# One set of 15 tiles for depthwise sums and products, TensorE's conv in bands 1, 3, 5 of the first six, and places of their own for the first two bands

## The chip, the cores and the metric

The kernel runs on one core of one Trainium2 chip. Five engines work side by side, each with a queue of its own that is executed in order: TensorE (PE, with weight loads shown apart as PEld), VectorE (DVE), ScalarE (ACT), GpSimd (POOL) and SyncE (SP); 16 DMA engines move data. The metric is the device time of one execution in microseconds, the median of the runs.

## What is computed

One block of an image transformer: a channel attention per image and a feed-forward part with a depthwise 3x3 convolution, both behind a layer norm over the channels, both added to their input. x is 16 images of 128 channels and 96 x 96 pixels, float32; HID is 512.

```python
def _attention(xn, wq, wk, wv, wp):
    q, k, v = xn @ wq.T, xn @ wk.T, xn @ wv.T      # split into 8 heads of 16 channels
    q, k = _l2norm(q), _l2norm(k)                  # over the pixels
    attn = softmax(einsum('bhcn,bhdn->bhcd', q, k) * scale, axis=-1)
    out = einsum('bhcd,bhdn->bhcn', attn, v)
    return out @ wp.T

def _ffn(xn_nchw, w_in, w_dw, w_out):
    h1 = einsum('bchw,oc->bohw', xn_nchw, w_in[:, :, 0, 0])
    h2 = conv3x3_depthwise(h1, w_dw, padding=1)    # 512 channels, a 3x3 kernel for each
    h3 = gelu(h2, approximate=False)
    return einsum('bchw,oc->bohw', h3, w_out[:, :, 0, 0])

x = x + _attention(_layernorm(x, ln1_w, ln1_b))
x = x + _ffn(_layernorm(x, ln2_w, ln2_b))
```

## The kernel before

**Tiling.** Channels lie on the 128 partitions. An image is cut into 24 units of four rows (384 pixels, three tiles of 128 pixels), 12 loads of eight rows, and 6 bands of 16 rows; there are 96 bands in all. The hidden 512 channels are four chunks of 128 (n = 0 to 3).

**Norms and attention.** Each norm transposes tiles of 128 pixels (L635), takes statistics on DVE (L642), variance and power -0.5 on POOL (L649, L653), for the second norm a shift on DVE (L657), normalises from PSUM into zT (L689, L693, ACT; for the first tiles of the first image half of it on DVE, L676, L680) and transposes back (L740) into a ring of rows, `xn` (L744, L746). The first norm also sums a Gram matrix (L703), from which `attention` makes one 128 x 128 matrix per image. The second norm of an image starts with `x2`: a matmul with that matrix (mix, L584), a copy with a bias (mixed, L593), and a DMA that adds the image's input (L596, add_x); the result is stored to the output (store_x2, L599, on SP).

**Feed-forward.** For each band and chunk there is a job (`conv_job`): hidden rows by matmuls in chunks of four or five rows (L915), copied from PSUM by ACT (kept, L918; the two rows shared with the next band by halo, L910); six of the nine taps on DVE, the first starting from the centre row (L939, tap); the two other taps as products on ACT (L932), each into a tile `pr`, the second added to the first by an accumulating DMA and the sum to the job's h3 tile by another (both L946, add_last and add_first, issued by POOL); then a GELU on ACT (L950). The last job of the kernel does all its taps on DVE. In 45 of the 96 bands the chunk n = 3 is not such a job: PE computes it straight from the ring with nine matmuls per strip of four rows (`by_matmuls`, L1004, conv), and ACT takes the GELU from PSUM (L1010, conv_gelu). Which bands these are is said by `by_pe`; in the first image they are bands 0, 2 and 4. `ffn_out` multiplies each strip of the four h3 tiles with w_out (L1028, out). ACT copies the sum into the h3 tile of chunk 3 (L1038, evicted), and a DMA adds it to the output (L1042, add_out); in the last two bands DVE adds it in SBUF instead (L1035, add) and SP stores it (L1052).

**What sets the order.** The instructions are not issued in the order of the loops. Every operation is entered in a `Plan` with its engine, an assumed duration, a place (a number in units of jobs: where it belongs by its band or pixel, plus an offset by kind from the table `AT`; the suffix `_0` marks offsets for the first image), and its reads and writes. `Plan.order` then plays the program through: whenever an engine is free, of its ready operations for which there is buffer space the one with the lowest place is taken. The order of starts is the order in which the instructions are written into the engines' queues. Since the offsets reach hundreds of jobs (the kernel has 339), most of them work as a rank among the kinds of an engine. `SLACK`, `WAIT`, `T_ADD` and `T_MOVE` are assumed latencies and transfer times: an accumulating DMA is taken to occupy the DMA engines for T_ADD[0] + rows * T_ADD[1] ns, one after the other.

**Buffers.** Pools are counted in the plan: two PSUM tiles for transposes (tr), four PSUM banks (h) for hidden, conv, mix and out, ten tiles h3 and five tiles pr of 128 x 1536 float32 (6 KB on each partition), four x tiles (xb), three x1. A pool named in IN_TURN gives its buffers only in the order of the places of the operations that take them first; in another pool any ready operation takes a free one.

Of the kernel before, what the change touches and what calls it, by code (L numbers as in the profile page):

```python
# [18 lines left out]
BR = 16  # L19
# [4 lines left out]
PE_LAST = (0, 1, 3, 4)  # L24
TINY = 1e-20
# [6 lines left out]
X1_BUFS, XB_BUFS, PR_BUFS, H3_BUFS, ZT_BUFS = 3, 4, 5, 10, 3  # L32
X0_BUFS = 3
LAST_ADDS = 2
IN_TURN = ("tr", "h3", "pr", "xb", "x1")
AT = dict(
    load_1=-82.1, load_2=-27.85, tables=-170.8, weights=-129.7, zeros=-5.45, load_a=-119.45, forth_a=-5.4,
    stats_a=-130.1, variance_a=-36.15, power_a=-38.2, scaled_a=-151.9, gram=7.8, back_a=-100.3, place_a=-166.4,
    attention=-123.25, mix=-101.45, residual=124.95, mixed=-106.55, add_x=-178.75, forth_b=-9.85,
    stats_b=-312.0, variance_b=594.35, power_b=241.0, shift_b=-51.85, scaled_b=-63.5, back_b=3.3, place_b=-6.65,  # L40
    evicted=-118.4, add_out=244.25, halo=-36.95, hidden=4.7, kept=-139.55, products=-75.8, add_last=43.35,
    tap=6.95, add_first=132.2, gelu=234.35, conv=3.75, conv_gelu=5.75, out=8.15, add=-100.45, store=85.05,
    mix_0=-101.6, residual_0=-64.15, mixed_0=101.1, add_x_0=77.55, gram_0=-52.6, forth_a_0=-54.45,
    forth_b_0=-9.0, stats_a_0=-275.15, stats_b_0=-308.15, scaled_a_0=-213.65, scaled_b_0=-68.05, back_a_0=-91.7,
    back_b_0=-101.3, place_a_0=-91.65, place_b_0=135.9, shift_b_0=-192.4, late=27.25, store_x2=34.35,
    store_x2_0=129.2, variance_a_0=-27.2, variance_b_0=76.25, power_a_0=-38.75, power_b_0=-6.8,
    attention_0=-133.2, load_a_0=-414.85,
)
STEP = dict(scaled=0.3, hidden=0.1, products=0.5, tap=0.166, conv=1.6, conv_tap=0.03, out=0.8, out_part=0.05)
SLACK = dict(PE=200, DVE=0, ACT=150, POOL=0, ADD=890, MOVE=800)  # L50
# [6 lines left out]
T_ADD, T_MOVE = (460.32, 221.76), 121  # L57
# [157 lines left out]
def tile_restormer_block(  # L215
# [171 lines left out]
    def add(p, f, r, w, n=BR):  # L387
        op("POOL", 800, p, f, r, w, 350 + SLACK["ADD"], dma=T_ADD[0] + n * T_ADD[1])
# [505 lines left out]
    def conv_job(j, g, n):  # L894
# [34 lines left out]
        def product(t):  # L929
            o0, o1 = reach(t)  # L930
            d["pr", t] = prp.tile([P, BR, W], F32, tag="pr", name=f"pr_{g}_{n}_{t}")
            nc.scalar.activation(d["pr", t][:, o0:o1, :], shifted(t, o0, o1), AF.Copy, scale=ratio[:, n, t : t + 1])  # L932
# [24 lines left out]
        for k, (r, e) in enumerate(chunks):  # L957
            ph = ("h", (jn, r))
            jk, zs = j + STEP["hidden"] * k, z_units(i, r0 - 1 + r, r0 - 1 + e)
            to = [("h1", n, k)]  # L960
            if r < 2:
                to.append(("h1", n, "first"))
            if e > BR:
                to.append(("h1", n, "last"))
            pe(t_mm((e - r) * W), at("hidden", jk), lambda r=r, e=e: hidden(r, e), [*zs, ("w", "in")], [ph])
            act(t_copy((e - r) * W), at("kept", jk), lambda r=r, e=e: kept(r, e), [ph], to)
        for k, t in enumerate(dma_taps):
            jk = j + STEP["products"] * k
            act(t_act(BR * W, 1), at("products", jk), lambda t=t: product(t), h1, [("pr", (jn, t))])
        pr = [("pr", (jn, t)) for t in dma_taps]  # L970
        for k, t in enumerate(dma_taps[1:]):
            add(at("add_last", j), lambda t=t: add_products(t), [pr[1 + k]], [pr[0]])
        for k, t in enumerate(left):
            o0, o1 = reach(t)
            dve(t_dve((o1 - o0) * (W if k == 0 or t % 3 == 1 else W - 1)), at("tap", j + STEP["tap"] * k), lambda t=t: tap(t), [*h1, ("w", "pads")], h3, True)
        if dma_taps:
            add(at("add_first", j), lambda: add_products(dma_taps[0]), [pr[0]], h3)
        if to_halo:
            act(t_copy(2 * W) + 44, at("halo", j), halo, [("h1", n, "last")], [("h1", n, "first")])
        for s in range(0, UPB, 1 if last else UPB):  # L980
            e = s + 1 if last else UPB
            act(t_act((e - s) * UT), at("gelu", j), lambda s=s, e=e: gelu(s, e), [], h3[s:e])

    def by_matmuls(p, g, s):
# [27 lines left out]
        for k, t in enumerate(order):  # L1012
            o0, o1 = reach(t)
            zs = z_units(i, r0 + o0 + t // 3 - 1, r0 + o1 + t // 3 - 1)
            ns = t_mm((o1 - o0) * (W - (t % 3 != 1)))
            pe(ns, at("conv", p + STEP["conv_tap"] * k), lambda t=t: product(t), [*zs, ("w", "conv")], [pc])
        act(t_act(UT), at("conv_gelu", p), gelu, [pc], [("h3", (g, PE_CHUNK), s)])

    def ffn_out(p, g, s):
# [34 lines left out]
        for k, n in enumerate(order):  # L1054
            pk = p + STEP["out_part"] * k
            pe(t_mm(UT), at("out", pk), lambda k=k, n=n: product(k, n), [("h3", (g, n), s), ("w", "out")], [po])
        if g < NG - LAST_ADDS:
            act(t_copy(UT), at("evicted", p), evicted, [po], [("h3", (g, PE_CHUNK), s)])
# [11 lines left out]
    def by_pe(g):  # L1070
        k = NG - 1 - g
        return k in PE_LAST if k < NB else (k + 1) * PE_SHARE[0] // PE_SHARE[1] > k * PE_SHARE[0] // PE_SHARE[1]
# [14 lines left out]
    for i in range(B):  # L1087
        start2 = job_of(NB * i - 1)
        end1 = start2 - NORM1_END
        start1 = job_of(NB * (i - 1)) if i else end1 - 8  # L1090
# [40 lines left out]
```

## Time and profile before

| | |
|---|---|
| time, median of 3 runs | 4080.88 us (4080.79 to 4082.98) |
| the profiled execution | 4089.63 us, of which the traced span is 4087.9 us |
| mean granted TensorE clock | 0.998 |
| DMA moved | 829.50 MB, mean 203 GB/s |

Groups of instructions are shown as "line engine op, output<-input, shapes, count | busy us in total, mean ns of one | idle time of the engine just before them, and what ended most of it". Matmuls of float32 are two instructions each; a busy PE is not PE at its peak, since their ends are modelled. In a timeline each row is a start, a length, an engine and a run of like instructions; a bracket gives idle time just before it and what ended that. An idle engine that doesn't set the pace costs nothing.

### The profile page before, as it was taken

What the parts mean: (1) busy time and instruction counts of PE and PEld (TensorE: products, weight loads), DVE (VectorE), ACT (ScalarE), POOL (GpSimd) and SP (SyncE); (2) the same over time, 40 slices, a digit from 0 to 9 for tenths busy, and PEclk for the clock granted to TensorE, in tenths of its full rate; (3) what the DMA queues carried; (4) which work ended last, traced back from release to release, by engine and by line L of the source; (5) the groups of instructions that cost most, each with busy time, mean ns of one, the idle gap of its engine ahead of it and who ended that gap; (6) DMA issues with size and microseconds to landing.
All of it is one profiled execution on the core that took longest, in us unless ns stands there. A gap on an engine that the chain in (4) does not pass through costs nothing. (4 is left out here: it accounts for less than half of the span.)

```text
span 4087.9 us, 50655 instructions
## 1 busy us (share of the span) xinstructions
PE 4025.0 (98%) x17209; PEld 2631.0 (64%) x17209; DVE 3967.9 (97%) x3773; ACT 3586.6 (88%) x6678; POOL 2659.8 (65%) x2166
## 2 busy tenths in 40 slices
PE   8999999999999999999999999999999999999999
PEld 6666666566666665666666666666666666666665
DVE  5999999999999999999999999999999999999999
ACT  5989989898899989988989898998989989899974
POOL 4657757576675767857677575765757757576631
PEclk9999999999999999999999999999999999999999
DMA  4989999998999999999999999999999999999987
GB/s 127 205 180 220 199 223 208 194 221 186 214 209 207 219 189 230 200 204 220 185 229 198 207 217 201 216 202 202 221 194 221 205 216 212 194 218 191 215 168 151
DMA packets 196291, 829.50 MB, mean 203 GB/s; under 512 B 22720, under 2 KB 24256, under 8 KB 196032
## 3 DMA queue, kind: packets, MB, share of 16 engines
q0 software_dynamic: 138096, 674.43, 85.0%
q1 hardware_dynamic: 55584, 151.02, 10.3%
q8 instruction: 137, 2.24, 0.2%
q10 hardware_dynamic: 2352, 0.81, 0.1%
q14 instruction: 122, 1.00, 0.1%
HBM read 150.62 MB, written 149.42 MB: 73 GB/s over the span
## 5 line engine op out<-in xcount | busy, mean ns | idle before, releaser
L939 DVE SCALAR_TENSOR_TENSOR h<-h,ratio,h 128x1520 f32<-128x1520 f32 (+1 forms) x1697 | 2988.1, 1779 | 3.6
L1004 PE MATMUL h<-xn,comp 128*128 128x380 f32 (+3 forms) x3294 | 1144.5, 477 | 2.8 <-ACT xn L744 0.9
L1028 PE MATMUL h<-h,woutT 128*128 128x384 f32 x3072 | 1126.5, 488 | 7.2 <-ACT h L918 3.7
L932 ACT ACTIVATE pr<-h,ratio 128x1536 f32<-128x1536 f32 (+1 forms) x676 | 1079.6, 1603 | 19.6 <-DMA h<-pr 10.6
L915 PE MATMUL h<-xn,winT 128*128 128x384 f32 (+3 forms) x2698 | 1052.7, 494 | 6.3 <-ACT h L918 4.5
L1004 PEld LDWEIGHTS h<-xn,comp 128*128 128x128 f32 x3294 | 593.3, 190 | 334.0 <-issue 18.2
L1028 PEld LDWEIGHTS h<-h,woutT 128*128 128x128 f32 x3072 | 557.4, 190 | 350.7 <-issue 41.8
L918 ACT COPY h<-h 128x384 f32<-128x384 f32 (+1 forms) x1307 | 661.3, 537 | 108.3 <-PE h L915 97.1
L915 PEld LDWEIGHTS h<-xn,winT 128*128 128x128 f32 x2698 | 484.2, 190 | 277.3 <-issue 21.3
L939 DVE SCALAR_TENSOR_TENSOR h<-h,ratio 128x1536 f32<-128x1536 f32 x339 | 613.8, 1813 | 15.7 <-PE h L1028 9.4
L653 POOL TENSOR_TENSOR rstd_b<-ve_b,mhalf 128x4 f32<-128x4 f32 x288 | 588.6, 2044 | 14.3
L653 POOL TENSOR_TENSOR rstd_a<-ve_a,mhalf 128x4 f32<-128x4 f32 x288 | 563.4, 1956 | 14.6
L649 POOL TENSOR_SCALAR ve_a<-st_a 128x4 f32<-128x4 f32 x288 | 369.1, 1282 | 292.9 <-DVE st_a L642 226.6
L950 ACT ACTIVATE h<-h 128x1536 f32<-128x1536 f32 x342 | 520.9, 1524 | 24.7 <-DMA h<-pr 23.1
L649 POOL TENSOR_SCALAR ve_b<-st_b 128x4 f32<-128x4 f32 x288 | 386.7, 1343 | 218.4 <-DVE st_b L642 196.9
L946 POOL DMA_DIRECT2D h<-pr x338 | 328.8, 973 | 293.0 <-DVE h L939 98.2
L946 POOL DMA_DIRECT2D pr<-pr x338 | 310.7, 920 | 296.6 <-ACT pr L932 255.2
L693 ACT ACTIVATE zT<-pT_b,nb_b,rstd_b 128x128 f32<-128x128 f32 x1132 | 433.2, 487 | 39.1 <-DVE nb_b L657 38.4
L689 ACT ACTIVATE zT<-pT_a,rstd_a 128x128 f32<-128x128 f32 x1080 | 319.4, 415 | 33.5 <-POOL rstd_a L653 32.6
L703 PE MATMUL g<-zT 128*128 128x129 f32 x2304 | 306.5, 276 | 0.0
L703 PEld LDWEIGHTS g<-zT 128*128 128x128 f32 x2304 | 289.1, 192 | 23.6 <-ACT zT L689 0.4
L584 PE MATMUL h<-xn,mwT 128*128 128x384 f32 x768 | 281.8, 491 | 7.5 <-ACT x L593 3.0
(172 smaller groups left out, 3660.0 us busy)
## 6 DMA issues: line engine op xcount, KB each, us to landing
h<-pr POOLq DMA_DIRECT2D x338, 768.0 KB, 10.3
pr<-pr POOLq DMA_DIRECT2D x226, 768.0 KB, 7.8
pr<-pr POOLq DMA_DIRECT2D x112, 720.0 KB, 14.1
x<-in_x_dram SPq DMA_DIRECT2D x192, 384.0 KB, 7.5
out_dram<-x SPq DMA_DIRECT2D x190, 384.0 KB, 10.1
x<-in_x_dram POOLq DMA_DIRECT2D x189, 384.0 KB, 11.9
out_dram<-h POOLq DMA_DIRECT2D x94, 768.0 KB, 10.6
out_dram<-x SPq DMA_DIRECT2D x4, 192.0 KB, 1.9
```

The source lines that it names most:

```text
L649: nc.gpsimd.tensor_scalar(ve, d["mv"][:, :, 2], 1.0 / C, EPS, ALU.mult, ALU.add)
L653: nc.gpsimd.tensor_tensor(rstd, d["ve"], mhalf, ALU.pow)
L693: nc.scalar.activation(zT(q)[:, k, :P], d["pT", q][:, k, :], AF.Identity, bias=d["nb"][:, t : t + 1], scale=d["rstd"][:, t : t + 1],)
L703: nc.tensor.matmul(grams[i][:, : P + 1], lhsT=zt[:, :P], rhs=zt, start=(q == 0 and k == 0), stop=(q == NU * TPU // QT - 1 and k == QT - 1),)
L915: nc.tensor.matmul(rows(ph)[:, k : k + m, :], lhsT=winT[:, n, :], rhs=z, start=True, stop=True)
L918: nc.scalar.copy(window(h1_, r, e - r, 1), rows(d.pop(("ph", r))))
L932: nc.scalar.activation(d["pr", t][:, o0:o1, :], shifted(t, o0, o1), AF.Copy, scale=ratio[:, n, t : t + 1])
L939: nc.vector.scalar_tensor_tensor(h3[:, o0:o1, w0:w1], shifted(t, o0, o1, w0, w1), ratio[:, n, t : t + 1], onto, ALU.mult, ALU.add)
L946: nc.gpsimd.dma_start(out=to[:, o0:o1, :], in_=d["pr", t][:, o0:o1, :], accum_op=ALU.add)
L950: nc.scalar.activation(h3, h3, AF.Gelu)
L1004: nc.tensor.matmul(d["pc"][:, o0 + k : o0 + k + m, w0:w1], lhsT=comp[:, t, :], rhs=z[:, :, w0 + dx : w1 + dx], start=(t == order[0]), stop ...
L1028: nc.tensor.matmul(rows(d["po"]), lhsT=woutT[:, n, :], rhs=h3s[g, n][:, s * UR : (s + 1) * UR, :], start=(k == 0), stop=(k == NCH - 1),)
```

## The change

It has four parts.

- In the first image PE's conv takes chunk 3 of bands 1, 3 and 5 in place of 0, 2 and 4 (`PE_FIRST`). The number of jobs stays 339.
- The pool of five pr tiles and that of ten h3 tiles become one pool of 15 h3 tiles, and it is no longer given out in the order of places.
- Nearly all offsets in `AT` change, and the feed-forward operations of the first two bands (g < HEAD) get offsets of their own with the suffix `_0`.
- The plan's assumptions change: SLACK of ACT, of accumulating DMAs (ADD) and of SP's transfers (MOVE), T_ADD, and 1000 ns in place of 800 for POOL's issue of an accumulating DMA.

No operation is added or removed.

```diff
 PE_CHUNK = 3
 PE_SHARE = (9, 20)
 PE_LAST = (0, 1, 3, 4)
+PE_FIRST = [1, 3, 5]
+HEAD = 2
+LATE1 = 0.0
 TINY = 1e-20
 UNIT_MIN = 1e-18
 DMA_TAPS = (1, 7)
...
 CENTRE = 4
 QT, QB = 4, 1
 H_BANKS = 4
-X1_BUFS, XB_BUFS, PR_BUFS, H3_BUFS, ZT_BUFS = 3, 4, 5, 10, 3
+X1_BUFS, XB_BUFS, PR_BUFS, H3_BUFS, ZT_BUFS = 3, 4, 1, 15, 3
 X0_BUFS = 3
 LAST_ADDS = 2
-IN_TURN = ("tr", "h3", "pr", "xb", "x1")
+IN_TURN = ("tr", "xb", "x1")
 AT = dict(
-    load_1=-82.1, load_2=-27.85, tables=-170.8, weights=-129.7, zeros=-5.45, load_a=-119.45, forth_a=-5.4,
-    stats_a=-130.1, variance_a=-36.15, power_a=-38.2, scaled_a=-151.9, gram=7.8, back_a=-100.3, place_a=-166.4,
-    attention=-123.25, mix=-101.45, residual=124.95, mixed=-106.55, add_x=-178.75, forth_b=-9.85,
-    stats_b=-312.0, variance_b=594.35, power_b=241.0, shift_b=-51.85, scaled_b=-63.5, back_b=3.3, place_b=-6.65,
-    evicted=-118.4, add_out=244.25, halo=-36.95, hidden=4.7, kept=-139.55, products=-75.8, add_last=43.35,
-    tap=6.95, add_first=132.2, gelu=234.35, conv=3.75, conv_gelu=5.75, out=8.15, add=-100.45, store=85.05,
-    mix_0=-101.6, residual_0=-64.15, mixed_0=101.1, add_x_0=77.55, gram_0=-52.6, forth_a_0=-54.45,
-    forth_b_0=-9.0, stats_a_0=-275.15, stats_b_0=-308.15, scaled_a_0=-213.65, scaled_b_0=-68.05, back_a_0=-91.7,
-    back_b_0=-101.3, place_a_0=-91.65, place_b_0=135.9, shift_b_0=-192.4, late=27.25, store_x2=34.35,
-    store_x2_0=129.2, variance_a_0=-27.2, variance_b_0=76.25, power_a_0=-38.75, power_b_0=-6.8,
-    attention_0=-133.2, load_a_0=-414.85,
+    load_1=117.1, load_2=143.85, tables=-90.8, weights=18.65, zeros=101.15, load_a=-110.6, forth_a=-4.4,
+    stats_a=-54.7, variance_a=-15.2, power_a=121.8, scaled_a=-832.95, gram=7.8, back_a=-123.35, place_a=78.25,
+    attention=-115.7, mix=-2.85, residual=-48.0, mixed=-106.15, add_x=-52.8, forth_b=-9.5, stats_b=-178.0,
+    variance_b=-93.15, power_b=-47.35, shift_b=90.8, scaled_b=-166.1, back_b=-51.15, place_b=-212.9,
+    evicted=1.25, add_out=92.9, halo=34.6, hidden=4.7, kept=-294.4, products=307.15, add_last=75.85, tap=316.95,
+    add_first=-144.65, gelu=229.4, conv=3.75, conv_gelu=253.7, out=8.15, add=555.9, store=147.4, mix_0=-129.1,
+    residual_0=-149.05, mixed_0=-89.75, add_x_0=29.65, gram_0=-91.9, forth_a_0=-192.4, forth_b_0=-8.45,
+    stats_a_0=-99.25, stats_b_0=-42.7, scaled_a_0=133.65, scaled_b_0=75.55, back_a_0=21.3, back_b_0=-233.8,
+    place_a_0=267.85, place_b_0=69.05, shift_b_0=-143.8, late=-172.4, store_x2=51.6, store_x2_0=72.7,
+    variance_a_0=-138.3, variance_b_0=12.35, power_a_0=169.5, power_b_0=-18.55, attention_0=-140.55,
+    load_a_0=-272.4, hidden_0=4.4, kept_0=-89.45, products_0=420.1, tap_0=24.0, add_last_0=374.45,
+    add_first_0=538.6, gelu_0=117.7, conv_0=3.15, conv_gelu_0=85.25, out_0=8.15, evicted_0=71.15,
 )
 STEP = dict(scaled=0.3, hidden=0.1, products=0.5, tap=0.166, conv=1.6, conv_tap=0.03, out=0.8, out_part=0.05)
-SLACK = dict(PE=200, DVE=0, ACT=150, POOL=0, ADD=890, MOVE=800)
+SLACK = dict(PE=200, DVE=0, ACT=100, POOL=0, ADD=770, MOVE=920)
 NORM1_END = 6.0
 EARLY = 5
 WAIT = dict(POOL=700, SP=1800, ACT=1800)
 T_WEIGHTS = 3000
 T_VARIANCE = 250
 T_POWER = 1010
-T_ADD, T_MOVE = (460.32, 221.76), 121
+T_ADD, T_MOVE = (456.21, 219.78), 121
 
 
 class Plan:
...
         op("POOL", ns, p, f, r, w, ns + 33 + SLACK["POOL"])
 
     def add(p, f, r, w, n=BR):
-        op("POOL", 800, p, f, r, w, 350 + SLACK["ADD"], dma=T_ADD[0] + n * T_ADD[1])
+        op("POOL", 1000, p, f, r, w, 350 + SLACK["ADD"], dma=T_ADD[0] + n * T_ADD[1])
 
     def move(p, f, r, w, n=XR):
         op("SP", 60, p, f, r, w, 350 + SLACK["MOVE"], dma=n * T_MOVE)
...
 
         def product(t):
             o0, o1 = reach(t)
-            d["pr", t] = prp.tile([P, BR, W], F32, tag="pr", name=f"pr_{g}_{n}_{t}")
+            d["pr", t] = h3p.tile([P, BR, W], F32, tag="h3", name=f"pr_{g}_{n}_{t}")
             nc.scalar.activation(d["pr", t][:, o0:o1, :], shifted(t, o0, o1), AF.Copy, scale=ratio[:, n, t : t + 1])
 
         def tap(t):
...
                 to.append(("h1", n, "first"))
             if e > BR:
                 to.append(("h1", n, "last"))
-            pe(t_mm((e - r) * W), at("hidden", jk), lambda r=r, e=e: hidden(r, e), [*zs, ("w", "in")], [ph])
-            act(t_copy((e - r) * W), at("kept", jk), lambda r=r, e=e: kept(r, e), [ph], to)
+            pe(t_mm((e - r) * W), at("hidden", jk, g >= HEAD), lambda r=r, e=e: hidden(r, e), [*zs, ("w", "in")], [ph])
+            act(t_copy((e - r) * W), at("kept", jk, g >= HEAD), lambda r=r, e=e: kept(r, e), [ph], to)
         for k, t in enumerate(dma_taps):
             jk = j + STEP["products"] * k
-            act(t_act(BR * W, 1), at("products", jk), lambda t=t: product(t), h1, [("pr", (jn, t))])
-        pr = [("pr", (jn, t)) for t in dma_taps]
+            act(t_act(BR * W, 1), at("products", jk, g >= HEAD), lambda t=t: product(t), h1, [("h3", ("pr", jn, t))])
+        pr = [("h3", ("pr", jn, t)) for t in dma_taps]
         for k, t in enumerate(dma_taps[1:]):
-            add(at("add_last", j), lambda t=t: add_products(t), [pr[1 + k]], [pr[0]])
+            add(at("add_last", j, g >= HEAD), lambda t=t: add_products(t), [pr[1 + k]], [pr[0]])
         for k, t in enumerate(left):
             o0, o1 = reach(t)
-            dve(t_dve((o1 - o0) * (W if k == 0 or t % 3 == 1 else W - 1)), at("tap", j + STEP["tap"] * k), lambda t=t: tap(t), [*h1, ("w", "pads")], h3, True)
+            dve(t_dve((o1 - o0) * (W if k == 0 or t % 3 == 1 else W - 1)), at("tap", j + STEP["tap"] * k, g >= HEAD), lambda t=t: tap(t), [*h1, ("w", "pads")], h3, True)
         if dma_taps:
-            add(at("add_first", j), lambda: add_products(dma_taps[0]), [pr[0]], h3)
+            add(at("add_first", j, g >= HEAD), lambda: add_products(dma_taps[0]), [pr[0]], h3)
         if to_halo:
             act(t_copy(2 * W) + 44, at("halo", j), halo, [("h1", n, "last")], [("h1", n, "first")])
         for s in range(0, UPB, 1 if last else UPB):
             e = s + 1 if last else UPB
-            act(t_act((e - s) * UT), at("gelu", j), lambda s=s, e=e: gelu(s, e), [], h3[s:e])
+            act(t_act((e - s) * UT), at("gelu", j, g >= HEAD), lambda s=s, e=e: gelu(s, e), [], h3[s:e])
 
     def by_matmuls(p, g, s):
 
...
             o0, o1 = reach(t)
             zs = z_units(i, r0 + o0 + t // 3 - 1, r0 + o1 + t // 3 - 1)
             ns = t_mm((o1 - o0) * (W - (t % 3 != 1)))
-            pe(ns, at("conv", p + STEP["conv_tap"] * k), lambda t=t: product(t), [*zs, ("w", "conv")], [pc])
-        act(t_act(UT), at("conv_gelu", p), gelu, [pc], [("h3", (g, PE_CHUNK), s)])
+            pe(ns, at("conv", p + STEP["conv_tap"] * k, g >= HEAD), lambda t=t: product(t), [*zs, ("w", "conv")], [pc])
+        act(t_act(UT), at("conv_gelu", p, g >= HEAD), gelu, [pc], [("h3", (g, PE_CHUNK), s)])
 
     def ffn_out(p, g, s):
         i, b = divmod(g, NB)
...
 
         for k, n in enumerate(order):
             pk = p + STEP["out_part"] * k
-            pe(t_mm(UT), at("out", pk), lambda k=k, n=n: product(k, n), [("h3", (g, n), s), ("w", "out")], [po])
+            pe(t_mm(UT), at("out", pk, g >= HEAD), lambda k=k, n=n: product(k, n), [("h3", (g, n), s), ("w", "out")], [po])
         if g < NG - LAST_ADDS:
-            act(t_copy(UT), at("evicted", p), evicted, [po], [("h3", (g, PE_CHUNK), s)])
+            act(t_copy(UT), at("evicted", p, g >= HEAD), evicted, [po], [("h3", (g, PE_CHUNK), s)])
             if s == UPB - 1:
                 cs = range(b * BR // XR, (b + 1) * BR // XR)
                 add(at("add_out", p), add_out, [("h3", (g, PE_CHUNK), k) for k in range(UPB)], [("o", i, c) for c in cs])
...
 
     def by_pe(g):
         k = NG - 1 - g
+        if g < NB:
+            return g in PE_FIRST
         return k in PE_LAST if k < NB else (k + 1) * PE_SHARE[0] // PE_SHARE[1] > k * PE_SHARE[0] // PE_SHARE[1]
 
     jobs, first = [], []
...
     for i in range(B):
         start2 = job_of(NB * i - 1)
         end1 = start2 - NORM1_END
-        start1 = job_of(NB * (i - 1)) if i else end1 - 8
+        start1 = job_of(NB * (i - 1)) + (LATE1 if i == 1 else 0) if i else end1 - 8
         norm(i, False, lambda t: start1 + (end1 - start1) * t / (NU * TPU))
         attention(at("attention", start2, i), i)
         norm(i, True, lambda t: start2 + band * t / TPB)
```

## The prediction

> **What bounds the kernel now.** I read the page's engine rows first, then the busy time of the engines in five stretches and two short ones near the end (columns: window, length, then PE, PEld, DVE, ACT and POOL busy with instruction counts, granted clock, DMA share, GB/s).
>
> ```profile
> PE 4025.0 (98%) x17209; PEld 2631.0 (64%) x17209; DVE 3967.9 (97%) x3773; ACT 3586.6 (88%) x6678; POOL 2659.8 (65%) x2166
> ```
>
> ```profile
> 0.00:60.00 60.00, 47.49 (x334) 43.25 (x335) 35.92 (x129) 22.42 (x65) 24.73 (x76) 0.95 0.39 113
> 60.00:100.00 40.00, 37.13 (x164) 23.64 (x164) 22.65 (x48) 28.00 (x59) 19.46 (x27) 0.99 0.61 144
> 100.00:3950.00 3850.00, 3810.19 (x16299) 2487.84 (x16298) 3780.90 (x3517) 3459.07 (x6449) 2595.45 (x2041) 1.00 0.98 207
> 3950.00:4050.00 100.00, 98.52 (x317) 57.89 (x316) 99.93 (x59) 69.43 (x98) 17.53 (x21) 1.00 0.84 162
> 4050.00:4088.00 38.00, 31.71 (x100) 18.39 (x98) 28.46 (x23) 7.67 (x10) 2.59 (x3) 1.00 0.52 119
> ```
>
> ```profile
> 3800.00:3900.00 100.00, 100.00 (x374) 61.68 (x373) 98.84 (x96) 86.60 (x157) 71.16 (x55) 1.00 1.02 215
> 3900.00:3950.00 50.00, 50.00 (x180) 30.96 (x179) 41.84 (x34) 41.90 (x66) 24.04 (x20) 1.00 0.92 182
> ```
>
> Three resources are nearly full at once from 100 to 3950 us: PE is idle for 3850 - 3810.2 = 39.8 us, DVE for 3850 - 3780.9 = 69.1 us, and the DMA engines are busy 0.98. The change keeps the number of PE's bands (three of the first six, 45 of 96 in all), so all three keep their work, and what can be won is idle time only: those 39.8 us of PE, the start (12.5 us of PE idle to 60, 2.9 to 100, but 17.4 of DVE in 60 to 100) and 6.3 us of PE at the end. From 3900 to 3950 DVE is idle 8.2 us beside a full PE, so close to the end it is PE that sets the pace.
>
> Then the waits (engine and line, what it waited for: total us, times, longest).
>
> ```profile
> POOL pr L946 <- ACT pr L932: 255.2, 127, 11.1
> ACT zT L693 <- DVE nb_b L657: 38.4, 46, 3.2
> ACT h L950 <- DMA h<-pr: 23.1, 10, 13.5
> DVE nb_b L657 <- POOL rstd_b L653: 21.7, 26, 1.9
> ACT pr L932 <- DMA h<-pr: 10.6, 13, 2.2
> DVE h L939 <- PE h L1028: 9.4, 4, 5.0
> ACT pr L932 <- DMA pr<-pr: 6.7, 10, 1.6
> ```
>
> The idle time is in small pieces. Waits for a buffer are the last three: products waiting for one of five product tiles (10.6 + 6.7 us of ACT) and first taps waiting until the output matmuls gave back an h3 tile (9.4 us of DVE). The one steady loss that POOL's order makes on DVE is the 21.7 us for rstd_b.
>
> The duration rows used below:
>
> ```profile
> L939 DVE SCALAR_TENSOR_TENSOR h<-h,ratio,h 128x1520 f32<-128x1520 f32 (+1 forms) x1697 | 2988.1, 1779 | 3.6
> L932 ACT ACTIVATE pr<-h,ratio 128x1536 f32<-128x1536 f32 (+1 forms) x676 | 1079.6, 1603 | 19.6 <-DMA h<-pr 10.6
> L653 POOL TENSOR_TENSOR rstd_b<-ve_b,mhalf 128x4 f32<-128x4 f32 x288 | 588.6, 2044 | 14.3
> L946 POOL DMA_DIRECT2D h<-pr x338 | 328.8, 973 | 293.0 <-DVE h L939 98.2
> ```
>
> **The change, part by part.** First, bands 1, 3, 5 instead of 0, 2, 4 for PE's conv. Band 0 gains a fourth DVE job: six taps of about 1.78 us (10.7 us of DVE), two products (3.2 us of ACT), two accumulating DMAs (two issues of 0.97 us on POOL), four more hidden matmul pairs. It gives up 36 conv matmuls of two instructions each, which band 1 takes; the same swap is made between bands 2 and 3 and between 4 and 5. The sum is nil; the place is not. From the timelines of PE, ACT and DVE at the start:
>
> ```profile
> 75.81 1.78 PE L1004 MATMUL h<-xn,comp 128*128 128x384 f32 x6
> 86.90 0.97 PE L915 MATMUL h<-xn,winT 128*128 128x480 f32 x2
> 88.77 2.20 PE L915 MATMUL h<-xn,winT 128*128 128x384 f32 x6 [0.46 <-ACT h L1010]
> ```
>
> ```profile
> 69.08 0.58 ACT L744 ACTIVATE xn<-pB_b,b 128x384 f32<-128x384 f32 x1
> 70.39 0.58 ACT L744 ACTIVATE xn<-pB_b,b 128x384 f32<-128x384 f32 x1
> 72.49 0.57 ACT L744 ACTIVATE xn<-pB_b,b 128x384 f32<-128x384 f32 x1
> 74.55 0.57 ACT L744 ACTIVATE xn<-pB_b,b 128x384 f32<-128x384 f32 x1
> 78.12 0.58 ACT L744 ACTIVATE xn<-pB_b,b 128x384 f32<-128x384 f32 x1 [0.15 <-PE pB_b L740]
> 89.98 0.61 ACT L744 ACTIVATE xn<-pB_b,b 128x384 f32<-128x384 f32 x1
> 96.35 0.69 ACT L744 ACTIVATE xn<-pB_b,b 128x384 f32<-128x384 f32 x1
> ```
>
> ```profile
> 91.77 1.82 DVE L939 SCALAR_TENSOR_TENSOR h<-h,ratio 128x1536 f32<-128x1536 f32 x1 [2.66 <-ACT h L918]
> ```
>
> A job of band 0 needs z rows 0 to 17, five units of four rows; the fifth L744 ends at 78.12 + 0.58 = 78.7. Yet PE's first hidden matmul starts at 86.9, behind conv matmuls of band 0 that began at 75.81, and its second chunk waits for the bank that the conv's GELU (L1010) reads. The first tap follows 4.87 us after the first hidden matmul. Without the conv in front, the same chain from 78.7 gives a first tap at 83.6: DVE, and with it the first products and DMAs, start 8.2 us earlier. That is the gain's end. The other end: PE loses the filler that it had before 100 us, L1004 for 12.21 us:
>
> ```profile
> 60.00:100.00 40.00, 12.21 (x36) 0.99 0.61 144
> ```
>
> What covers it is hidden work of band 0 (four jobs of four chunks, some 10.5 us, by 0.97 + 2.20 us in the rows above for a first job with its waits) and the conv strips of band 1 as their units arrive. If that cover fails, 12.2 us are lost. Since PE, not DVE, paces the end, a head start of DVE counts in part only: -3, between -8.2 and +12.2.
>
> Second, the end. Only two bands keep their output sums in SBUF, added by DVE (L1035). Those adds had place -100 and now have 555.9, behind the taps' 316.95.
>
> ```profile
> 4059.51 0.55 DVE L1035 TENSOR_TENSOR x<-h,x 128x384 f32<-128x384 f32 x1
> 4066.82 0.55 DVE L1035 TENSOR_TENSOR x<-h,x 128x384 f32<-128x384 f32 x1
> 4068.90 0.55 DVE L1035 TENSOR_TENSOR x<-h,x 128x384 f32<-128x384 f32 x1
> 4072.69 0.55 DVE L1035 TENSOR_TENSOR x<-h,x 128x384 f32<-128x384 f32 x1
> 4073.16 7.05 DVE L939 SCALAR_TENSOR_TENSOR h<-h,ratio,h 128x1425 f32<-128x1425 f32 x4
> 4081.81 1.85 DVE L1035 TENSOR_TENSOR x<-h,x 128x384 f32<-128x384 f32 x3 [1.61 <-PE h L1028]
> ```
>
> Four adds stand between the last job's taps, each pushing the next tap by about 0.47 us (4059.51 to 4059.98 in start times); moved behind the taps, they fill the gap of 1.61 us before 4081.81. That saves 4 x 0.47 = 1.9 us. The wait it can add: a sum that isn't added holds one of four PSUM banks, and PE's last output matmuls queue behind it. Bounds: the whole PE idle time after 4050, -6.3, and the same again lost. I take -2.
>
> Third, one set of 15 tiles, taken by whoever is ready, not in the order of places. It can remove the three buffer waits. ACT's 17.3 us lie beside 12% of idle ACT time and are worth nothing alone; DVE's 9.4 us are worth up to themselves. What it can add: products made early may hold tiles that first taps want, and the tap, its later taps, the GELU and the output matmuls stand behind it. One such wait is 9.4 / 4 = 2.35 us; one in every tenth of the 339 jobs would be 34 x 2.35 = 80 us, the other end. I take -4, since 15 shared tiles admit every split that 10 and 5 did.
>
> Fourth, the places. On POOL the variance of the second norm goes from last (594) to near the front (-93), its power from 241 to -47, and the first norm's power goes last (121.8). This works on the 21.7 us of DVE and, through nb_b, on the 38.4 us of ACT. The first-add DMAs move from 132 to the very front (-144.65). Each waits for a job's last tap, and variances, powers and the other DMAs stand behind it in POOL's queue, with ACT's normalising behind those; but a place chooses among ready operations only, so this costs where the chip is later than the plan, and POOL is idle a third of the time. On ACT the products go from the middle (-75.8) to last (307); the accumulating DMAs, the taps' completion and the GELU come after them. Bounds: -21.7 from POOL's order; for ACT's order, DMA share falling from 0.98 to 0.97 over 3850 us, 39 us. I take -6, nearer to nothing, because the products' lateness shows today only on POOL (255.2 us), which has slack. On PE the mix goes from -101.45 to -2.85 and the back transposes of the second norm from 3.3 to -51.15: the same instructions later or earlier among others that keep PE full, so nothing. SP keeps its order, loads ahead of stores. The planner's own numbers (slack, transfer times, 1000 ns instead of 800 per issue beside 973 ns measured) issue nothing and act through the order alone.
>
> **Sum.** -3 - 2 - 4 - 6 = -15 us on the profiled execution's 4089.63 us (span 4087.9), so 4074.6. The median of the runs, 4080.88, lies 8.75 us below the profiled time; the same offset gives 4066.
>
> A rule of the Trainium skill speaks to the first term (Perfetto Trace Analysis, Identifying the Most-Contended Engine): TensorE's headroom is judged by weight-load busy time, not by matmul busy time. By it PE at 64% would have a third to spare, DVE would be the bound, and the whole head start of 8.2 us would count: 4061. The trace shows what 64% is here:
>
> ```profile
> 4063.22 13.06 PE L1028 MATMUL h<-h,woutT 128*128 128x384 f32 x40
> L1028 PEld LDWEIGHTS h<-h,woutT 128*128 128x128 f32 x3072 | 557.4, 190 | 350.7 <-issue 41.8
> ```
>
> 40 matmuls without a gap take 13.06 us, 0.33 us each, with one load of 0.19 us each: 58% load share in a stretch where PE is full. So I keep -3.
>
> **Rivals.** (a) Larger gain: shared tiles and POOL's order remove half of the steady idle time. Half of PE's 39.8 us is 20, with 8 at the start and 2 at the end 30: 4051. For it, the waits are short and many; against it, they have many causes, of which the change touches four.
>
> (b) No change: band 0's lost filler shows in full and PE carries it to the end. The first part then costs its +12.2 us, the other three give -12: 4081. For it: PE paces the end. Against it: before 60 us PE was idle 12.5 us anyway for the chain of the first image, and the sixth and seventh units, which open the first two strips of band 1's conv, were there at 90.6 and 97.0 us already. A second mechanism lends it something: powers run faster while no taps run,
>
> ```profile
> 65.00 1.01 POOL L653 TENSOR_TENSOR rstd_b<-ve_b,mhalf 128x4 f32<-128x4 f32 x1
> ```
>
> against 2.04 us on average. Taps that start earlier slow the four batches that band 1's units 5 to 8 need (tiles 15 to 26, four to a batch) by 1.03 us each: 4.1 us later z rows, and by this alone 4066 + 4 = 4070, inside the forecast's own range. The Trainium skill names this as a lock on a port pair shared by VectorE and GpSimd, for VectorE instructions with two SBUF inputs too (SBUF — State Buffer, SBUF: two separate sides). It speaks against starting taps earlier, and the two durations agree with it.
>
> (c) Slower: ACT's products at the back of its queue. DMA is the third full resource and is fed only through products, which now yield to each gather of GELUs, evictions and norm scalings. Point from which it decides: the DMA share from 100 to 3950 falls by 0.01 or more without the span having been bound elsewhere; each 0.01 is 38.5 us. One hundredth, with 5 us of start and end gained: 4114. For it: ACT is 90% busy there, so last in its order means long delays, and POOL waits for products 127 times already. Against it: five tiles of lead become up to fifteen.
>
> **Chances.** Forecast (4055 to 4073) 0.40, (a) 0.17, (b) 0.18, (c) 0.25. This kernel can tell 0.2%, 8.2 us: faster is below 4072.7 and slower above 4089.0. Forecast and (a) are faster, 0.57; (b) is the same, 0.18; (c) is slower, 0.25. The likeliest case's own range is 4055 to 4073. To leave out no more than two in ten I go down to 4040, past (a)'s value, and up to 4108, most of the way to one lost hundredth of DMA share.
>
> **What would show it.** First part: first L939 at or before 85 us, first L1004 after 85. Second: no L1035 between the last job's taps. Third: DVE h waiting for PE h L1028 near nothing, and no new wait of DVE for an output or a transfer. Fourth: DVE nb_b waiting for rstd_b well below 21.7, DMA share still 0.98. Together: PE idle from 100 to 3950 below 30 us. A DMA share of 0.97, or more than 69 us of DVE idle there, would prove me wrong.

## The result, and the profile after

The changed kernel takes 4129.37 us (median of 4 runs, 4127.2 to 4136.93) beside 4080.84 us for the kernel before in the same runs: a ratio of 1.0123, with a 95% interval of 1.0106 to 1.0141. It is 48.5 us slower, where 15 us faster was forecast, and lies above the stated range, which ended at 4108. Its profiled execution took 4128.37 us, of which the span is 4126.6.

The engine row of the page and the busy time by stretches of the kernel after (windows placed as before, the end later):

```profile
PE 4046.3 (98%) x17209; PEld 2638.8 (64%) x17209; DVE 3968.6 (96%) x3773; ACT 3586.9 (87%) x6678; POOL 2595.2 (63%) x2166
```

```profile
0.00:60.00 60.00, 48.29 (x322) 42.18 (x323) 37.20 (x132) 20.16 (x59) 24.49 (x76) 0.89 0.38 113
60.00:100.00 40.00, 37.69 (x164) 23.69 (x163) 30.14 (x50) 32.78 (x67) 23.10 (x25) 0.96 0.66 159
100.00:3950.00 3850.00, 3787.93 (x16164) 2470.52 (x16163) 3737.34 (x3484) 3423.06 (x6392) 2508.12 (x2026) 1.00 0.97 205
3950.00:4090.00 140.00, 139.28 (x460) 82.86 (x459) 139.79 (x91) 104.78 (x154) 37.00 (x39) 1.00 0.87 167
4090.00:4127.00 37.00, 33.08 (x105) 19.50 (x103) 24.18 (x20) 6.16 (x9) 2.51 (x3) 1.00 0.50 117
```

The work is the same (instruction counts agree on every engine). The start is better: DVE is idle 9.9 us from 60 to 100, not 17.4. The time is lost in the long middle stretch: there DVE is idle 3850 - 3737.3 = 112.7 us (69.1 before) and PE 62.1 us (39.8 before). PE's busy time over the whole run has grown by 21 us with the same matmuls, and the granted clock was lower (0.993 on average, 0.998 before): 4126.6 x 0.007 less 4087.9 x 0.002 is 21 us of clock, the same amount. The loss is not spread evenly. Two windows hold a good part of it:

```profile
2000.00:2100.00 100.00, 93.09 (x333) 55.88 (x333) 91.44 (x83) 84.32 (x141) 47.78 (x43) 0.95 1.02 215
...
2900.00:3000.00 100.00, 90.70 (x398) 60.80 (x398) 88.63 (x83) 81.45 (x157) 60.63 (x51) 0.95 0.93 202
```

The waits of DVE and of ACT's products in the kernel after say what is new (L943 is the tap, L936 the product, L646 the statistics, L639 the transpose before them, L661 the shift nb_b; they were L939, L932, L642, L635 and L657):

```profile
DVE st_b L646 <- PE pT_b L639: 28.7, 42, 3.8
...
ACT pr L936 <- DMA pr<-pr: 23.2, 11, 6.7
DVE st_a L646 <- PE pT_a L639: 22.5, 25, 7.2
...
DVE h L943 <- DMA h<-pr: 14.8, 6, 6.2
...
DVE nb_b L661 <- POOL rstd_b L657: 11.5, 15, 1.9
...
DVE h L943 <- DMA pr<-pr: 9.1, 3, 6.1
```

Before, no tap ever waited for a DMA. Now nine do, for 23.9 us in all. The products' waits for DMAs between product tiles (pr<-pr) have grown from 6.7 to 23.2 us, and the longest from 1.6 to 6.7. One of the taps' waits shows what such a wait drags along. POOL's, DVE's, ACT's and PE's timelines around 2064 us of the kernel after:

```profile
2059.01 0.92 POOL L950 DMA_DIRECT2D pr<-pr  x1 [0.43 <-ACT pr L936]
```

```profile
2064.66 1.82 DVE L943 SCALAR_TENSOR_TENSOR h<-h,ratio 128x1536 f32<-128x1536 f32 x1 [6.08 <-DMA pr<-pr]
2066.40 1.79 DVE L943 SCALAR_TENSOR_TENSOR h<-h,ratio,h 128x1520 f32<-128x1520 f32 x1
2068.11 0.15 DVE L661 SCALAR_TENSOR_TENSOR nb_b<-st_b,rstd_b 128x4 f32<-128x4 f32 x1
```

```profile
2068.30 1.50 ACT L697 ACTIVATE zT<-pT_b,nb_b,rstd_b 128x128 f32<-128x128 f32 x4 [3.14 <-DVE nb_b L661]
```

```profile
2068.81 0.82 PE L744 MATMUL pB_b<-ident,zT 128*128 128x128 f32 x2 [2.06 <-ACT zT L697]
```

A first tap waits 6.08 us for a DMA issued at 2059.01. Behind it in DVE's queue, after one more tap, stands the small shift nb_b. For that, ACT's normalisation waits 3.14 us, and for the normalisation PE waits 2.06 us.

A product's wait drags along as much. Two of them, and the matmul on PE that came next, from the timelines of ACT and PE in the kernel after:

```profile
2375.91 1.50 ACT L936 ACTIVATE pr<-h,ratio 128x1440 f32<-128x1440 f32 x1 [5.02 <-DMA pr<-pr]
2377.91 1.65 PE L919 MATMUL h<-xn,winT 128*128 128x384 f32 x2 [4.57 <-ACT h L922]
```

```profile
2927.86 1.57 ACT L936 ACTIVATE pr<-h,ratio 128x1536 f32<-128x1536 f32 x1 [6.72 <-DMA pr<-pr]
2930.51 1.11 PE L639 MATMUL pT_b<-ident,x 128*128 128x128 f32 x4 [7.20 <-ACT zT L693]
```

Behind such a product in ACT's queue stand the copies (L922) and normalisations (L693) for which PE waits. A third case ends at 2676.51, with a wait of 5.56 us on ACT and of 4.54 us on PE. These are the three longest pauses of PE from 100 to 3950 us, 16.3 us together, where PE's idle time there has grown by 22 us.

Why should a first tap wait for a DMA that reads a product tile? A tap writes a fresh h3 tile. Which memory it gets is decided in two places: the plan counts free tiles by the time at which it reckons their last user done, and the tile pool of the language then assigns the memory itself. Counted in the two built programs: before, all 1071 tiles of this kind follow the same tile in their memory as in the plan; after, 447 do not. For three first taps with a wait of 6 us (the 20th, the 168th, which is the one above, and the 239th):

```
first tap of     the plan: memory of     the program: memory of
h3, band 5, n 1     h3, band 3, n 0         pr, band 4, n 2
h3, band 47, n 0    h3, band 45, n 1        pr, band 47, n 0
h3, band 67, n 0    h3, band 65, n 0        pr, band 66, n 1
```

The tap of band 47 was given the memory of its own job's second product, whose accumulating DMA had just been issued; the plan had meant a tile freed long before. In 964 of 1056 cases the pool's choice is the free tile whose last user stands earliest in the program. So it goes, in nine cases of ten, by position in the program, where a DMA stands at its issue, and not by the time at which it lands. With ten h3 and five pr tiles apart and in the order of places, both rules gave the same answer; in one shared set they do not.

### The profile page after: what moved, and what is told of

It reads as the page before. It is cut to its first block, busy times and chain, and to the rows that moved or that the text cites. A ratio compares the mean times of both kernels' runs of the same rounds, so it can differ in the third digit from the quotient of the medians.

```text
span 4126.6 us, 50740 instructions
## 1 busy us (share of the span) xinstructions
PE 4046.3 (98%) x17209; PEld 2638.8 (64%) x17209; DVE 3968.6 (96%) x3773; ACT 3586.9 (87%) x6678; POOL 2595.2 (63%) x2166
## 4 chain that ended last, share of the span: by engine, by line
PE 68%; DVE 10%; ACT 10%; DMA 7%; POOL 3%; issue 2%; ACTq 0%; POOLq 0%; DVEq 0%
PE h L1008 18%; PE h L1032 17%; PE h L919 14%; DVE h L943 9%; PE g L707 5%; DMA pr<-pr 4%; PE h L588 3%; ACT pr L936 3%; DMA h<-pr 2%; PE pB_a L744 2%; PE pT_a L639 2%; PE pT_b L639 2%; PE pB_b L744 2%; ACT h L922 2%; ACT zT L697 1%
## 5 line engine op out<-in xcount | busy, mean ns | idle before, releaser
L943 DVE SCALAR_TENSOR_TENSOR h<-h,ratio,h 128x1520 f32<-128x1520 f32 (+1 forms) x1697 | 2987.7, 1779 | 3.1
L936 ACT ACTIVATE pr<-h,ratio 128x1536 f32<-128x1536 f32 (+1 forms) x676 | 1093.7, 1630 | 30.7 <-DMA pr<-pr 23.2
L922 ACT COPY h<-h 128x384 f32<-128x384 f32 (+1 forms) x1307 | 682.0, 556 | 159.2 <-PE h L919 145.5
L943 DVE SCALAR_TENSOR_TENSOR h<-h,ratio 128x1536 f32<-128x1536 f32 x339 | 613.9, 1813 | 37.1 <-DMA h<-pr 14.8
L657 POOL TENSOR_TENSOR rstd_b<-ve_b,mhalf 128x4 f32<-128x4 f32 x288 | 575.6, 1999 | 11.8
L657 POOL TENSOR_TENSOR rstd_a<-ve_a,mhalf 128x4 f32<-128x4 f32 x288 | 570.5, 1981 | 13.3
L950 POOL DMA_DIRECT2D h<-pr x338 | 318.0, 941 | 391.9 <-DVE h L943 272.0
L950 POOL DMA_DIRECT2D pr<-pr x338 | 326.1, 965 | 340.6 <-ACT pr L936 300.2
L653 POOL TENSOR_SCALAR ve_a<-st_a 128x4 f32<-128x4 f32 x288 | 360.2, 1251 | 274.7 <-DVE st_a L646 229.7
L653 POOL TENSOR_SCALAR ve_b<-st_b 128x4 f32<-128x4 f32 x288 | 363.2, 1261 | 229.8 <-DVE st_b L646 198.8
L693 ACT ACTIVATE zT<-pT_a,rstd_a 128x128 f32<-128x128 f32 x1080 | 324.2, 434 | 31.7 <-POOL rstd_a L657 31.2
L588 PE MATMUL h<-xn,mwT 128*128 128x384 f32 x768 | 298.3, 494 | 8.6 <-ACT x L597 4.7
```

The lines of the kernel that those rows point to most:

```text
L653: nc.gpsimd.tensor_scalar(ve, d["mv"][:, :, 2], 1.0 / C, EPS, ALU.mult, ALU.add)
L657: nc.gpsimd.tensor_tensor(rstd, d["ve"], mhalf, ALU.pow)
L922: nc.scalar.copy(window(h1_, r, e - r, 1), rows(d.pop(("ph", r))))
L943: nc.vector.scalar_tensor_tensor(h3[:, o0:o1, w0:w1], shifted(t, o0, o1, w0, w1), ratio[:, n, t : t + 1], onto, ALU.mult, ALU.add)
L950: nc.gpsimd.dma_start(out=to[:, o0:o1, :], in_=d["pr", t][:, o0:o1, :], accum_op=ALU.add)
```

## The experiments

Theory T1: this hand-out of the shared set makes the loss. Theory T2: the new places make it, the products at the end of ACT's order above all, which is rival (c) of the prediction.

**The plan's own tiles.** The changed kernel with the same order of instructions, each tile in the one of 15 fixed tiles that the plan meant:

```diff
-    h3p = ctx.enter_context(tc.tile_pool(name="h3p", bufs=H3_BUFS))
+    h3p = ctx.enter_context(tc.tile_pool(name="h3p", bufs=1))
+    own = [h3p.tile([P, BR * W], F32, name=f"own_{k}") for k in range(H3_BUFS)]
...
-            h3s[g, n] = h3p.tile([P, BR, W], F32, tag="h3", name=f"h3_{g}_{n}")
+            h3s[g, n] = rows(own[plan.slot["h3", (g, n)]])
...
-            d["pr", t] = h3p.tile([P, BR, W], F32, tag="h3", name=f"pr_{g}_{n}_{t}")
+            d["pr", t] = rows(own[plan.slot["h3", ("pr", jn, t)]])
```

> The changed kernel with the same 15 tiles, places, bands and order of instructions, but each h3, pr, weights and zT tile sits in the one of 15 fixed tiles that the plan gave it, instead of the one that the tile pool hands out. In the changed program 447 of 1071 tiles follow another tile in their memory than the plan had reckoned with. Theory T1 (the pool hands tiles out in the order in which their last users were issued, so a tap or a product gets a tile whose DMA is still under way): first taps no longer wait for DMAs (14.8 + 9.1 us before), ACT's products wait 10 us or less for pr<-pr (23.2), DVE idle from 100 to 3950 us falls from 112.7 to 75 or less, and the time to 4070 to 4095. Theory T2 (the new places, products last on ACT above all, lose the time whatever the memory): within 8 us of 4129.

Measured: 4088.87 us (10 runs), 40.5 us less than the changed kernel; against the kernel before, 1.0015 (1.0006 to 1.0025), a loss of 6 us. (Each taken beside the kernel before in its own runs, the difference is 48.5 - 6.3 = 42 us.) Its middle stretch and its waits:

```profile
100.00:3950.00 3850.00, 3813.42 (x16300) 2489.40 (x16299) 3777.34 (x3515) 3452.52 (x6441) 2532.47 (x2040) 1.00 0.98 206
```

```profile
DVE st_b L647 <- PE pT_b L640: 23.5, 41, 1.8
...
DVE st_a L647 <- PE pT_a L640: 14.1, 28, 2.5
...
ACT own L937 <- DMA own<-own: 3.6, 5, 1.2
...
DVE own L944 <- DMA own<-own: 0.4, 1, 0.4
```

All tiles are called own here, so the products' waits for these DMAs are one row: 3.6 us, from 23.2 (pr<-pr) and 3.7 (h<-pr). Taps' waits for DMAs fall from 23.9 to 0.4 us, DVE's idle time from 112.7 to 72.7, PE's longest pause from 7.2 to 2.2, and PE's busy time is 4029.8 us. T2 is out for all but the last 6 us.

**The old order with the pool's hand-out.** The kernel before, with its five and ten tiles drawn from one pool of 15; the plan still counts them apart, so the order is the old one:

```diff
-    h3p = ctx.enter_context(tc.tile_pool(name="h3p", bufs=H3_BUFS))
+    h3p = ctx.enter_context(tc.tile_pool(name="h3p", bufs=H3_BUFS + PR_BUFS))
...
-            d["pr", t] = prp.tile([P, BR, W], F32, tag="pr", name=f"pr_{g}_{n}_{t}")
+            d["pr", t] = h3p.tile([P, BR, W], F32, tag="h3", name=f"pr_{g}_{n}_{t}")
```

> The kernel before, order of instructions unchanged, with five pr and ten h3 tiles drawn from one pool of 15 by the tile pool's own rule, while the plan still counts them apart. T1: new waits of first taps and products for DMAs, 20 us or more slower, 4100 to 4140. T2: the order is the old one, so within 8 us of 4081.

Measured: 4115.28 us, 1.0084 (1.0068 to 1.0099), 33 us more than the kernel before. The taps' waits of this run show DMAs where there were none (11.4 us in three waits, and 4.3 us in three more for pr<-pr), and more waiting for ACT's copies (6.2 us before):

```profile
DVE h L939 <- ACT h L918: 17.6, 12, 4.7
...
DVE h L939 <- DMA h<-pr: 11.4, 3, 4.2
```

So the hand-out alone, with no new place, band or assumption, costs two thirds of the loss in another order.

**Control.** The kernel before with 15 fixed tiles by the plan's numbers (ten and five), the same edit as in the first experiment.

> Control: the kernel before with its ten h3 and five pr tiles as 15 fixed tiles by the plan's numbers. Nothing else is changed, and each tile follows the same tile in its memory as in the kernel before. T1: fixed tiles do nothing by themselves, within 8 us of the kernel before. If fixed tiles cost or win something of their own (other waits, other addresses), it shows here, and the reading of e1_own_tiles has to be corrected by it.

Measured: 4081.3 us, 0.9997 (0.9988 to 1.0006). Fixed tiles by themselves change nothing that can be told.

**The bands alone.** The kernel before with PE's conv in bands 1, 3, 5:

```diff
+        if g < NB:
+            return g in (1, 3, 5)
```

> The kernel before with PE's conv in bands 1, 3 and 5 of the first image, nothing else changed (places planned anew by the old table). By the prediction's first part: first tap at 85 us or earlier instead of 91.8, time 3 us lower, between 4073 and 4093. If the old places don't suit these bands: first tap unchanged, or PE idle at 60 to 130 us, and 4085 to 4095. T1 and T2 both leave this open.

Measured: 4105.02 us, 1.0056 (1.0039 to 1.0072), 22 us slower, which neither case had. The first tap came at 81.52 us, ten earlier, as the prediction reckoned. From 60 to 130 us PE was idle 7.1 us, where it had been idle 2.9; and DVE's waits for rstd_b grew from 21.7 to 36.4 us over the kernel. The start of this run in the 60 to 130 us window, with the kernel before below it:

```profile
60.00:130.00 70.00, 62.86 (x272) 38.84 (x271) 59.17 (x76) 60.81 (x119) 42.90 (x42) 1.00 0.82 184
```

```profile
60.00:130.00 70.00, 67.13 (x296) 43.62 (x296) 52.58 (x73) 56.07 (x112) 36.20 (x40) 0.99 0.74 166
```

In the old places the conv was filler, as the prediction feared. That is about 4 us of PE; where the rest of the 22 us comes from is not shown. A plan made anew shifts everything behind the edit, so this run cannot be read as the price of one move.

**The old bands in the new places.** The first experiment with `PE_FIRST = [0, 2, 4]`.

> As e1_own_tiles, with PE's conv in bands 0, 2 and 4 again. If the earlier first tap (81.2 instead of 91.8 us) is worth what DVE gains at the start, this is 8 to 11 us slower than e1_own_tiles; if PE's work paces the kernel, within 4 us of it.

Measured: 4092.56 us, 1.0026 (1.0015 to 1.0037) to the kernel before, 3.7 us more than with the new bands, with intervals that overlap. The first tap falls back from 79.4 to 90.3 us. So an early start of 11 us comes with a gain of about a third of itself, which is not clear of the noise. The plan was made anew here too, so this also compares two orders and is not the price of one move. What became of the head start is seen in DVE's timeline at the end of the first experiment's run:

```profile
4060.71 0.55 DVE L1040 TENSOR_TENSOR x<-h,x 128x384 f32<-128x384 f32 x1
...
4065.30 0.56 DVE L1040 TENSOR_TENSOR x<-h,x 128x384 f32<-128x384 f32 x1 [0.70 <-PE h L1033]
4065.78 3.56 DVE L944 SCALAR_TENSOR_TENSOR own<-h,ratio,own 128x1536 f32<-128x1536 f32 x2
4069.26 0.55 DVE L1040 TENSOR_TENSOR x<-h,x 128x384 f32<-128x384 f32 x1
4070.46 0.56 DVE L1040 TENSOR_TENSOR x<-h,x 128x384 f32<-128x384 f32 x1 [0.66 <-PE h L1033]
4073.04 0.56 DVE L1040 TENSOR_TENSOR x<-h,x 128x384 f32<-128x384 f32 x1 [2.02 <-PE h L1033]
```

in PE's there:

```profile
4062.52 18.22 PE L1033 MATMUL h<-own,woutT 128*128 128x384 f32 x56
```

and in the last taps and the middle stretch of the run with the old bands:

```profile
4066.18 7.04 DVE L944 SCALAR_TENSOR_TENSOR own<-h,ratio,own 128x1425 f32<-128x1425 f32 x4
```

```profile
100.00:3950.00 3850.00, 3812.78 (x16284) 2491.01 (x16283) 3784.45 (x3515) 3452.65 (x6441) 2535.12 (x2038) 1.00 0.98 206
```

The last tap ends at 4069.3 us with the new bands and at 4073.2 with the old ones, so 3.9 us of the 11 are left. Between, DVE is idle 72.7 us with the new bands and 65.6 with the old: most of the head start went as idle time in the middle. With either bands the last tap ends well before the end of the span, by 15.0 and 18.5 us (7.7 in the kernel before). What ends the run is 56 output matmuls without a gap, from 4062.5 to 4080.7 us in the first experiment, and DVE waits for their sums.

**Places fitted anew.** With fixed tiles 6 us remained between the changed kernel and the kernel before. The question was whether the plan's new assumptions are too short. Two kernels as in the first experiment, with the old assumptions (but for the 1000 ns per issue, which stay) and two different tables of places fitted to them:

```diff
-SLACK = dict(PE=200, DVE=0, ACT=100, POOL=0, ADD=770, MOVE=920)
+SLACK = dict(PE=200, DVE=0, ACT=150, POOL=0, ADD=890, MOVE=800)
...
-T_ADD, T_MOVE = (456.21, 219.78), 121
+T_ADD, T_MOVE = (460.32, 221.76), 121
```

> The changed kernel with fixed tiles, the latencies, slack and transfer times that the plan of the kernel before assumed, and places fitted anew to these. If what is left of e1_own_tiles against the kernel before comes from assumptions that are too short (ACT 100 for 150, accumulating DMAs 770 for 890), this is 8 to 20 us faster than e1_own_tiles, 4065 to 4081, at or under the kernel before. If not, within 6 us of e1_own_tiles, 4083 to 4095.

> As e7_own_replanned_a with another fit of the places; it tells how far the result hangs on one table of places. Both theories as there; the two within 8 us of each other.

Measured: 4070.89 us, 0.9970 (0.9958 to 0.9982), and 4069.92 us, 0.9970 (0.9958 to 0.9981): both faster than either kernel, and 18 us under the first experiment. That looked like the assumptions. The opposite test went from these two tables back to the short assumptions, with the places fitted on until the plan's own end was that of the changed kernel:

> e7_own_replanned_a with the changed kernel's assumptions in the plan (ACT 100, accumulating DMAs 770, SP's transfers 920, T_ADD 456.21 and 219.78), and its places fitted on to these until the plan's own end is that of the changed kernel. Fixed tiles. If the short assumptions lose the time between e1_own_tiles and e7_own_replanned_a (18 us): 4080 to 4095, with more waits of ACT and DVE for DMAs and for ACT's results than e7. If it was the one table of places: within 6 us of 4071.

> The same step from e8_own_replanned_b (4069.9 us) with another fit: 4080 to 4095 if the short assumptions lose the time, within 6 us of 4070 if not.

Measured: 4075.31 us, 0.9979 (0.9970 to 0.9987), and 4070.31 us, 0.9966 (0.9954 to 0.9978). The short assumptions do not lose the time, so that theory fell: between these two kernels and the first experiment nothing differs but the table of places. Where the last of these is better than the first experiment is seen in its middle stretch and its waits for transposes, as the 23.5 + 14.1 us there are 8.9 + 8.3 us here:

```profile
100.00:3950.00 3850.00, 3826.55 (x16386) 2508.30 (x16385) 3798.99 (x3531) 3468.30 (x6477) 2571.46 (x2049) 1.00 0.98 207
```

```profile
DVE nb_b L663 <- POOL rstd_b L659: 16.0, 19, 2.0
...
DVE st_b L648 <- PE pT_b L641: 8.9, 21, 1.0
...
DVE st_a L648 <- PE pT_a L641: 8.3, 23, 1.5
```

In all four the products keep the last rank among the kinds on ACT that recur in every image, so that rank alone does not lose the 6 us either. Which of the other places makes the difference was not tried one by one, since a single place moved changes the whole plan.

**The hand-out once more.** The order of the first of these four (4070.89 us) with the 15 tiles handed out by the pool again; 478 of 1071 tiles then follow another than the plan reckons with.

> The order of instructions of e7_own_replanned_a (4070.9 us), with the 15 tiles handed out by the tile pool again, so that 478 of 1071 tiles follow another tile than the plan reckons with. T1: first taps and products wait for DMAs again, 25 to 55 us slower than e7_own_replanned_a, 4095 to 4126. If the hand-out only hurt the one order of the changed kernel: within 10 us of 4071.

Measured: 4125.04 us, 1.0099 (1.0082 to 1.0116): 54 us for the hand-out in this order. First taps wait 14.1 and 7.4 us for DMAs again, products 22.9 us for pr<-pr. DVE's idle time from 100 to 3950 us is 3850 - 3741.4 = 108.6 us with it and 3850 - 3794.1 = 55.9 us without:

```profile
100.00:3950.00 3850.00, 3790.09 (x16172) 2476.30 (x16170) 3741.42 (x3486) 3422.61 (x6397) 2530.03 (x2027) 0.99 0.97 205
```

```profile
100.00:3950.00 3850.00, 3827.54 (x16372) 2502.69 (x16371) 3794.08 (x3526) 3467.72 (x6466) 2562.10 (x2045) 1.00 0.98 207
```

The new places cannot be had with ten and five tiles apart: in these places the plan finds no order for that split, its operations lock each other out of tiles.

## Why the prediction was wrong

**The step that failed is the third**, one set of 15 tiles. It was taken at -4 "since 15 shared tiles admit every split that 10 and 5 did". That counts tiles and does not ask which one an operation gets. The measured term is +40.5 us (the changed kernel against its own order with fixed tiles), and the same step costs 33 and 54 us in two other orders. The step's other bound named a kindred mechanism, taps held up by products that hold tiles, and priced it at 2.35 us a wait and 80 us in all. The taps' waits for DMAs were nine, of up to 6.2 us and 23.9 in all, and shifts, normalisations and transposes stood behind them. The step also put the waits of ACT's products at nothing, because ACT is idle for 12% of the time. That failed too: eleven waits for pr<-pr of up to 6.7 us hold up whatever stands behind them in ACT's queue, and PE's three longest pauses (7.20, 4.57 and 4.54 us) stand behind such waits. How the 40.5 us divide between taps and products was not measured apart.

**The first part was right in time; its worth is not settled.** The first tap was forecast at 83.6 us and came at 81.20. The loss of filler did not show in the new places: PE was idle 2.3 us from 60 to 100, 2.9 before, with as many matmuls, though at a clock of 0.96 for 0.99. The head start was put at -3 of 8.2, because PE paces the end. With fixed tiles the difference was -3.7, between two orders and with overlapping intervals, so that the numbers agree is luck as far as these runs go. PE does pace the end; but DVE lost most of the head start in the middle, which the prediction did not reckon with. In the old places the same bands cost 22 us, more than the bound of +12.2. (The cover was given as some 10.5 us; four jobs at the 0.97 + 2.20 us beside it are 12.7.)

**The second part shows no worth.** The adds did not all go behind the taps: two still stand between taps in the first experiment, at 4060.7 and 4065.3 us. The part was not run by itself, but DVE's last tap ends 15 us before the end there, while PE runs 56 matmuls without a gap, so sooner taps had little to win. The prediction had read from 3900 to 3950 us that PE sets the pace, and did not apply it here.

**The fourth was right in one wait and wrong in sum.** DVE's wait for rstd_b fell from 21.7 to 11.5 us, and to 14.7 with fixed tiles, where -6 was taken. But statistics wait longer for transposes. In the kernel before it was

```profile
DVE st_b L642 <- PE pT_b L635: 19.2, 31, 3.2
...
DVE st_a L642 <- PE pT_a L635: 12.0, 23, 1.8
```

31.2 us; it is 51.2 in the changed kernel and 37.6 with fixed tiles. There the 7.0 us won on rstd_b stand against 6.4 lost here. The places as a whole, with the bands' gain in them, are worth +6 us (1.0015, 1.0006 to 1.0025), a small loss, where -11 was forecast for all but the third part. Other tables with the same tiles and bands came to between -8 and -13 us against the kernel before, so the size hangs on the table of places as a whole.

**Of the rivals,** (c) came nearest, with 4114 us and a DMA share that falls from 0.98 to 0.97, and it had the wrong cause. Its mark did show: the share is 0.97. With the same order and fixed tiles it is 0.98 again and the time is gone, so the lower share was the same bytes over a longer time. A mark that every cause of a loss would show tells nothing apart.

## What to carry to other kernels

A buffer count is not a buffer assignment: where a schedule is planned outside the tool that assigns memory, compare which tile follows which in memory with what the plan meant, or assign the tiles by the plan. Sharing one set between tiles that a DMA frees and tiles that an engine frees is where the two part, because a DMA is issued microseconds before it is done (here 5.6 us, from 2059.01 to the tap that it held up until 2064.66). And a head start is worth what is left of it at the end, on the engine that ends the run: here 3.9 of 11 us were left at the last tap, on an engine that then waited for another.

## What was not expected of the hardware

A short gap on PE can cost more than itself. Around the wait of 2.06 us that ends at 2068.81 the granted clock, in windows of one microsecond of the kernel after, was:

```profile
2067.00:2068.00 1.00, 0.00 (x0) 0.00 (x0) 1.00 (x1) 0.00 (x0) 0.00 (x0) 1.00 1.02 257
2068.00:2069.00 1.00, 0.19 (x1) 0.14 (x1) 1.00 (x3) 0.70 (x2) 0.00 (x0) 0.95 1.05 261
2069.00:2070.00 1.00, 0.78 (x3) 0.32 (x3) 1.00 (x2) 1.00 (x4) 0.00 (x0) 0.50 1.12 228
2070.00:2071.00 1.00, 1.00 (x5) 1.00 (x6) 1.00 (x2) 1.00 (x1) 0.00 (x0) 0.50 1.06 213
2071.00:2072.00 1.00, 1.00 (x2) 0.45 (x2) 1.00 (x2) 1.00 (x3) 0.00 (x0) 0.50 1.12 197
2072.00:2073.00 1.00, 1.00 (x4) 0.68 (x3) 1.00 (x3) 0.63 (x2) 0.68 (x2) 0.84 0.96 177
2073.00:2074.00 1.00, 1.00 (x4) 0.59 (x4) 1.00 (x2) 0.91 (x2) 1.00 (x2) 1.00 1.05 209
```

Half the clock from 2069 to 2072, with PE busy but for a fifth of the first microsecond, and 0.84 and 0.95 beside it: 3 x 0.50 + 0.16 + 0.05 = 1.7 us of clock, nearly as much again as the gap. Such stretches make up the 21 us by which PE's busy time is longer with the same matmuls, and they are one reason why the loss is greater than the waits themselves. The Trainium skill (TensorE: Matmul & The Clock Gate, Part 1: The HAM clock gate) puts the drop after an idle window of about 3.4 us and the return after as long a busy one; the return agrees here (matmuls again from 2068.81, the full clock within the microsecond from 2072), and the drop came after a shorter gap, of 2.06 us. Length alone does not decide: in the first experiment a gap of 2.21 us had no drop behind it. PE's timeline and the window around it:

```profile
2402.62 0.85 PE L745 MATMUL pB_a<-ident,zT 128*128 128x128 f32 x3 [2.21 <-ACT zT L694]
```

```profile
2399.00:2407.00 8.00, 5.79 (x27) 3.66 (x26) 6.43 (x7) 5.18 (x13) 5.87 (x5) 1.00 1.05 233
```

What decides is not shown by these runs.
